# Narrower weights in an attention kernel's value products

## The chip, the cores and the metric

The kernel runs on one core of a Trainium2 chip. The core has a matrix engine (TensorE; PE in the profile, with its weight loads listed apart as PEld), three engines for elementwise work (VectorE or DVE, ScalarE or ACT, GpSimd or POOL), and DMA queues that are fed from ScalarE (ACT) and SyncE (SP). Each engine runs its own list of instructions in order; semaphores order them against each other. The metric is the device time of one execution in microseconds; the median of several runs is compared.

## The reference

There are 16 graphs of 1024 nodes with 256 features and a 0/1 adjacency matrix. Layer 0 is multi-head attention with 8 heads of 32 features, with a leaky ReLU on the scores and the adjacency as mask:

```python
q = heads(features @ Wq); k = heads(features @ Wk); v = heads(features @ Wv)
e = jnp.einsum('whqd,whkd->whqk', q, k)
e = jnp.where(e >= 0, e, ALPHA * e)
attn = jax.nn.softmax(jnp.where(adj[:, None] > 0, e, NEG), axis=-1)
h = jnp.einsum('whqk,whkd->whqd', attn, v)
```

It is followed by a layer norm, a product of `[h, features]` with `Wffn`, another layer norm and a residual. Layer 1 is two graph attention steps (softmax over a sum of two per-node scores, masked by the same adjacency), a layer norm, a feed-forward network with 1024 hidden units, and a last layer norm. All is float32. The change concerns the last line above: weights times values.

## The kernel before

The queries and keys of a head are kept as rows of features, with nodes along the free dimension. Of the 1024 nodes, key tiles of 128 (`t`, 8 of them, `NT`) go on the partitions, and queries in two halves of 512 (`nh`, 2 of them, `NH`) go along the free dimension. The steps of one head are:

- `all_scores` (L576): for two key tiles at a time, 128 keys x 1024 queries of scores into PSUM (`ps_s`).
- `weights` (L594 to L603): `p` = leaky ReLU of the scores (ScalarE scales at L594, VectorE takes the maximum at L596, which also frees the PSUM buffer), its exponential (ScalarE, L599), and the product with the mask (GpSimd, L603). Nothing is subtracted before the exponential.
- `all_values` (L623), the changed step: for two key tiles at a time (`GV`), the values of 128 keys are the stationary operand (the weights of the array), `p` is the moving one, and the result is summed over the 8 key tiles in one PSUM buffer, `acc` (`ps_a` in the profile). There is one such buffer. Queries 0 to 511 land on its partitions from 0, queries 512 to 1023 on those from 64.
- `after_head` (L649 to L656): `acc` is copied to SBUF (`ho`), transposed in blocks of 128 x 128, and the 32 sums are divided by the 33rd.

The values lie in `v` with 33 columns per head (`VW` = `DH` + 1): 32 features and a constant column, so that the 33rd sum is the softmax's denominator (both are negated, and so is the mask). Four heads (`G`) share one `v`, and 31 columns of zeros follow the last of them:

```python
v = buf([P, NT, G * VW + 31], "v", "v")
nc.gpsimd.memset(v[:, :, G * VW:], 0.0)
```

The kernel before reads 64 columns from each head's first, so 31 of them belong to the next head or to the zeros. What they give lands on partitions 33 to 63 and 97 to 127 of `acc`. The copy and the transposes go over all 128 partitions; of the transposed columns only 0 to 32 of each 64 are used:

```python
src = pt.rearrange("p (i j c) -> p j i c", i=TPH, j=NH)
nc.vector.reciprocal(rd, src[:, :, :, DH])
```

The rest of a graph (`rows_pair`, `attention`, `second_rows`, `normed_pair`, `feed_forward`; among their products L847, L872, L912 and L940, and the graph step's exponentials L795 and L797) is worked off while the next graph's heads run, and fills TensorE between their scores and value products.

The order of all instructions is fixed when the program is built. Each piece of work is a thread that names its engine and an estimated cost; a planner (`Order`) picks the next thread by its due time (`aim`) among those that could start soon. The two value tiles of a batch are charged as one piece, `on(PE=240 + 860 * GV)`. Everything is float32; each float32 product of this kernel appears as two weight loads and two matmuls in the profile.

Of the kernel before, what the change touches and what calls it, by code (L numbers as in the profile page):

```python
# [177 lines left out]
def on(shared=False, delay=0.0, **costs):  # L178
    return "on", (costs, shared, delay)
# [6 lines left out]
def wait(event):  # L186
    return "wait", event
# [6 lines left out]
def take(pool):  # L194
    return "take", pool


def give(pool):
    return "give", pool


def start(thread, aim):
    return "start", (thread, aim)


def aim(time, lead):
    return "aim", (time, lead)
# [17 lines left out]
def unshifted_path(  # L225
# [8 lines left out]
    nc = tc.nc  # L234
# [10 lines left out]
    VW = DH + 1  # L245
# [307 lines left out]
    def pace(b):  # L553
        return PACE * {0: AIM["fast0"], 1: AIM["fast1"], B - 1: AIM["fast15"]}.get(b, 1.0)
# [51 lines left out]
    def all_values():  # L606
        for b in range(B):
            for h in range(H):
                g, c = h // G, (h % G) * VW
                for u in range(NP):  # L610
                    yield wait(("v", b, g, u))
                v = vs[b, g]
                yield take("acc")
                acc = psum.tile([P, HALF], FT, tag="acc", name="ps_a", bufs=bufs["acc"])
                for d in range(0, NT, GV):
                    for t in range(d, d + GV):
                        yield wait(("p", b, h, t))
                    yield aim(begin[b] + (h * NT + d + 2) / 2 * pace(b), SLOT)
                    yield on(PE=240 + 860 * GV)
                    for t in range(d, d + GV):  # L620
                        p = probs.pop((b, h, t))
                        for nh in range(NH):
                            nc.tensor.matmul(acc[nh * 64:(nh + 1) * 64, :], v[:, t, c:c + 64],  # L623
                                             p[:, nh * HALF:(nh + 1) * HALF],
                                             start=(t == 0), stop=(t == NT - 1))
                    for t in range(GV):
                        yield give("p")
                yield start(after_head(b, h, acc), begin[b] + (h + 1) * NT // 2 * pace(b))
                if h % G == G - 1:
                    yield give("v")  # L630
            yield start(rest(b), work.now)

    def after_head(b, h, acc):
        if h == 0:
            yield take("hn")
            hn[b] = buf([P, NT, D], "hn", "hn")
            checks[b] = small.tile([P, NSUM + NSCORE], FT, name="check", bufs=2)
            yield fire(("hn open", b))
        yield wait(("hn open", b))
        yield take("pair")  # L640
        ho = buf([P, HALF], "pair", "ho")
        engine = yield evacuate(HALF)
        copy(engine, ho, acc)
        yield give("acc")
        yield take("misc")
        pt = misc()
        yield on(PE=450)
        for i in range(TPH):
            nc.tensor.transpose(pt[:, i * P:(i + 1) * P], ho[:, i * P:(i + 1) * P], ident)  # L649
        yield give("pair")  # L650
        src = pt.rearrange("p (i j c) -> p j i c", i=TPH, j=NH)
        rd = checks[b][:, h * NT:(h + 1) * NT].rearrange("p (j i) -> p j i", j=NH)
        yield on(DVE=210)
        nc.vector.reciprocal(rd, src[:, :, :, DH])
        yield on(DVE=430)
        nc.vector.tensor_tensor(hn[b].rearrange("p (j i) d -> p j i d", j=NH)[:, :, :, h * DH:(h + 1) * DH],  # L656
                                src[:, :, :, :DH], rd[:, :, :, None].to_broadcast([P, NH, TPH, DH]), op=OP.mult)
        yield give("misc")
        yield fire(("hn", b, h))
# [304 lines left out]
    def rest(b):  # L964

        t0 = work.now

        def at(share):
            return t0 + share * SLOT

        for h in range(H):
            yield wait(("hn", b, h))
        yield take("w8")
        y1 = y1s[b] = buf([P, NT, YW], "w8", "y1")
        x1s[b] = dram.tile([NP, P, DC, 2 * P], FT, name="x1_kept")
        for q in range(NH):
            yield start(head_stats(b, q), at(0))
        for u in range(NP):
            yield start(rows_pair(b, u), at(AIM["rows"] + AIM["rows_step"] * u))
        for u in range(NP):  # L980
            yield wait(("hn used", b, u))
        yield give("hn")
        yield start(free_x(b), work.now)
        big = yield from attention(b, 0, y1, at)
        yield take("w8")
        y2 = buf([P, NT, YW], "w8", "y2")
        for i in range(NT):
            yield start(second_rows(b, big, y1, y2, i), at(AIM["second"] + AIM["second_step"] * i))
        for i in range(NT):
            yield wait(("row", b, 1, i))  # L990
        yield give("big")
        yield give("w8")
        for u in range(2):
            yield start(fetch_x1(b, u), at(AIM["normed"]))
        big = yield from attention(b, 1, y2, at)
        yield give("mask")
        yield start(count(b), at(1.0))
        for u in range(NP):
            yield start(normed_pair(b, u, big, y2), at(AIM["normed"] + AIM["normed_step"] * u))
        for u in range(NP):  # L1000
            yield wait(("weighed", b, u))
            if u + 2 < NP:
                yield start(fetch_x1(b, u + 2), at(AIM["normed"]))
        yield give("big")
        yield give("w8")
# [83 lines left out]
    with tc.manual_schedule():  # L1089
        for dst, w in ((wq, Wq), (wk, Wk), (wv, Wv)):  # L1090
            load_w(dst, w)
        work.add(project(0, -SLOT), 0.0)
        work.add(load_stacks(), 0.0)
        work.add(all_scores(), 0.0)
        work.add(all_values(), 0.0)
        work.add(prepare(), 0.5 * SLOT)
        work.run()
# [308 lines left out]
```

## Time and profile before

| | |
|---|---|
| median of three runs | 4535.08 us (4533.97 to 4536.34) |
| the profiled execution | 4533.21 us |
| its span, first to last instruction | 4531.4 us |
| mean granted TensorE clock | 0.987 |
| TensorE busy | 4348.7 us |
| VectorE, ScalarE, GpSimd busy | 3304.5, 2893.6, 2454.6 us |
| L623 matmuls (4096 records) | 1019.9 us busy, 615 ns mean |
| L623 weight loads (4096 records) | 246.1 us busy, 137 ns mean |

The profile is of one execution. Busy time counts a stretch once where records overlap. Matmuls are pipelined, and a record's end is modelled: the time that a matmul really takes from the engine is read from the distance between the starts of neighbouring records, not from the length of one. A weight load overlaps the matmuls that run beside it; what a load costs is again seen in the starts of the matmuls around it. The chain of waits is followed back from the last instruction, at each step to what released it or to the instruction before it on its engine. In lines of instructions, "128*64 128x512" stands for 128 rows and 64 columns of weights and a moving operand of 512 columns.

### The profile page before, as it was taken

To read this page: it belongs to the slowest core of one execution; us is meant where nothing else is said; L and a number is where in the kernel's file an instruction comes from. 1 tells how busy PE (TensorE), PEld (TensorE's weight loads), DVE (VectorE), ACT (ScalarE), POOL (GpSimd) and SP (SyncE) were. 2 spreads that over 40 slices of the span, in tenths; PEclk is the share of its full clock that TensorE was granted. 3 is DMA by queue.
4 is the path that set the end of the run, shared out by engine and by line. 5 is a ranking of instruction groups with operands and counts; after the bars stand their busy time and mean duration, and the time that the engine had idled before them with its cause. 6 is when DMAs were issued, how large, how long until landed. Compare 5 with 4: busy or idle time off the path is not lost.

```text
span 4531.4 us, 57125 instructions
## 1 busy us (share of the span) xinstructions
PE 4348.7 (96%) x20298; PEld 2924.8 (65%) x20298; DVE 3304.5 (73%) x5246; ACT 2893.6 (64%) x4030; POOL 2454.6 (54%) x1544
## 2 busy tenths in 40 slices
PE   6778999999999999999999999999999999999999
PEld 3345666767666676666767666676666767666587
DVE  4766778777787777768777787777768777776854
ACT  4556666666666666666676666666676676666631
POOL 3655565465565545655565565555655565565710
PEclk8899999999999999999999999999999999999999
DMA  5312223222232312323132232322323222231100
GB/s 173 106 49 70 82 70 101 62 79 81 62 98 63 105 54 75 96 59 110 54 89 75 59 98 67 103 64 70 89 64 105 63 86 68 60 99 49 34 22 20
DMA packets 159108, 343.57 MB, mean 76 GB/s; under 512 B 24672, under 2 KB 27232, under 8 KB 158816
## 3 DMA queue, kind: packets, MB, share of 16 engines
q1 hardware_dynamic: 112736, 255.93, 20.0%
q10 hardware_dynamic: 46080, 83.91, 6.2%
q8 instruction: 164, 2.69, 0.2%
q14 instruction: 128, 1.05, 0.1%
HBM read 239.09 MB, written 100.66 MB: 75 GB/s over the span
## 4 chain that ended last, share of the span: by engine, by line
PE 72%; DVE 15%; POOL 5%; issue 4%; ACT 2%; DMA 0%; ACTq 0%; POOLq 0%; SPq 0%; DVEq 0%
PE ps_a L623 16%; PE ps_s L576 10%; PE ps_m L872 8%; PE ps_m L847 8%; PE ps_m L912 7%; PE ps_m L940 7%; DVE att L810 5%; POOL p L603 5%; DVE att L813 5%; PE ps_m L460 3%; DVE p L596 3%; PE ps_m L757 3%; PE ps_m L725 2%; PE ps_m L728 2%; PE ps_m L351 2%
## 5 line engine op out<-in xcount | busy, mean ns | idle before, releaser
L603 POOL TENSOR_TENSOR p<-p,mask 128x1024 f32<-128x1024 f32 x1024 | 2212.3, 2177 | 1654.9 <-ACT p L599 1528.0
L596 DVE TENSOR_TENSOR p<-p,ps_s 128x1024 f32<-128x1024 f32 x1024 | 1209.9, 1213 | 403.0 <-ACT p L594 402.2
L599 ACT ACTIVATE p<-p 128x1024 f32<-128x1024 f32 x1024 | 1081.1, 1058 | 409.7 <-DVE p L596 380.5
L594 ACT ACTIVATE p<-ps_s 128x1024 f32<-128x1024 f32 x993 | 973.6, 1025 | 189.8 <-PE ps_s L576 169.0
L623 PE MATMUL ps_a<-p,v 128*64 128x512 f32 x4096 | 1019.9, 615 | 47.3 <-POOL p L603 45.1
L576 PE MATMUL ps_s<-qs,ks 128*128 128x512 f32 x2048 | 631.5, 428 | 37.2 <-DVE p L596 34.7
L623 PEld LDWEIGHTS ps_a<-p,v 128*64 128x64 f32 x4096 | 246.1, 137 | 536.7 <-issue 384.5
L576 PEld LDWEIGHTS ps_s<-qs,ks 128*128 128x128 f32 x2048 | 352.9, 191 | 331.8 <-DVE p L596 98.3
L872 PE MATMUL ps_m<-y,att 128*128 128x256 f32 x2048 | 483.2, 382 | 16.3 <-ACT v L497 13.6
L940 PE MATMUL ps_m<-wf,hid 128*128 128x256 f32 x2048 | 474.0, 381 | 9.4 <-ACT xT L309 8.7
L912 PE MATMUL ps_m<-rT,wf 128*128 128x256 f32 x2048 | 474.6, 381 | 4.0 <-ACT z L309 4.0
L847 PE MATMUL ps_m<-y,att 128*128 128x258 f32 x2048 | 472.3, 381 | 2.9 <-DVE hn L656 2.9
L872 PEld LDWEIGHTS ps_m<-y,att 128*128 128x128 f32 x2048 | 377.2, 190 | 81.9 <-ACT v L497 16.3
L940 PEld LDWEIGHTS ps_m<-wf,hid 128*128 128x128 f32 x2048 | 379.3, 190 | 78.2 <-issue 15.3
L847 PEld LDWEIGHTS ps_m<-y,att 128*128 128x128 f32 x2048 | 385.9, 190 | 66.7 <-issue 6.0
L912 PEld LDWEIGHTS ps_m<-rT,wf 128*128 128x128 f32 x2048 | 378.6, 191 | 52.7 <-ACT z L309 4.2
L810 DVE SCALAR_TENSOR_TENSOR att<-first,second 128x1024 f32<-128x1024 f32 x256 | 352.7, 1378 | 82.0 <-ACT first L797 82.0
L813 DVE SCALAR_TENSOR_TENSOR att<-mask,att 128x1024 f32<-128x1024 fp8e4 x256 | 329.8, 1288 | 8.7
L818 ACT ACTIVATE y<-y,check 128x258 f32<-128x258 f32 x256 | 130.8, 511 | 299.3 <-DVE check L816 277.7
L334 POOL TENSOR_SCALAR rs<-mv 128x2 f32<-128x2 f32 (+1 forms) x224 | 58.0, 259 | 392.4 <-DVE mv L331 392.3
L400 DVE TENSOR_SCALAR adj_b<-adj_i 128x512 fp8e4<-128x512 int32 x256 | 249.7, 1020 | 15.5 <-DMA adj_i<-in_adj_dram 15.5
L921 ACT ACTIVATE hid<-ps_m,bf 128x256 f32<-128x256 f32 x383 | 163.5, 472 | 130.6 <-PE ps_m L912 102.7
(100 smaller groups left out, 4254.2 us busy)
## 6 DMA issues: line engine op xcount, KB each, us to landing
adj_i<-in_adj_dram ACTq DMA_DIRECT2D x256, 256.0 KB, 3.4
qs<-qk_halves SPq DMA_DIRECT2D x256, 256.0 KB, 4.1
ks<-qk_halves SPq DMA_DIRECT2D x256, 256.0 KB, 5.1
qk_halves<-high SPq DMA_DIRECT2D x128, 256.0 KB, 3.2
qk_halves<-low SPq DMA_DIRECT2D x128, 256.0 KB, 3.7
xr<-in_x_dram ACTq DMA_DIRECT2D x64, 256.0 KB, 2.9
x_kept<-x SPq DMA_DIRECT2D x64, 256.0 KB, 2.0
x<-x_kept SPq DMA_DIRECT2D x64, 256.0 KB, 5.4
```

What stands on the lines that cost most here:

```text
L576: nc.tensor.matmul(ps[i][:, cols], kk[:, t * P:(t + 1) * P], q[:, cols], start=True, stop=True)
L594: nc.scalar.activation(p, ps, AF.Copy, scale=ALPHA)
L596: nc.vector.tensor_tensor(p, p, ps, op=OP.max)
L599: nc.scalar.activation(p, p, AF.Exp)
L603: nc.gpsimd.tensor_tensor(p, p, mask_of(b, t), op=OP.mult)
L623: nc.tensor.matmul(acc[nh * 64:(nh + 1) * 64, :], v[:, t, c:c + 64], p[:, nh * HALF:(nh + 1) * HALF], start=(t == 0), stop=(t == NT - 1))
L810: nc.vector.scalar_tensor_tensor(e, first[:, 0, :], second[:, j:j + 1], first[:, 1, :], op0=OP.mult, op1=OP.max)
L813: nc.vector.scalar_tensor_tensor(e, mask_of(b, j), -1.0, e, op0=OP.mult, op1=OP.mult, accum_out=sums[:, j:j + 1])
L847: nc.tensor.matmul(pa[:, cols:cols + width], big[:, j, i * P:(i + 1) * P], rows[:, j, :width], start=(j == 0), stop=(j == NT - 1))
L872: nc.tensor.matmul(pa[:, i * D:(i + 1) * D], big[:, j, t * P:(t + 1) * P], y2[:, j, :D], start=(j == 0), stop=False)
L912: nc.tensor.matmul(pa[:, i * 2 * P:(i + 1) * 2 * P], wf1[:, dc, hc * P:(hc + 1) * P], rT[:, dc, :], start=(dc == 0), stop=(dc == DC - 1))
L940: nc.tensor.matmul(pa[:, i * D:(i + 1) * D], hid[hc // 2][:, hc % 2, i * P:(i + 1) * P], wf2[:, hc, :], start=(hc == 0), stop=False)
```

## The change

The value product of a head's first key tile stays as it is, with 64 columns of `v` into 64 partitions. For the seven other key tiles it takes `VW` = 33 columns into 33 partitions. The partitions past the 33rd keep what the first tile's product, which begins the sum, put there, and are still copied and transposed. The two query halves keep their first partitions, 0 and 64. The cost that the planner is given is not changed, and the order of instructions is the same on every engine.

```diff
                     for t in range(d, d + GV):
                         p = probs.pop((b, h, t))
                         for nh in range(NH):
-                            nc.tensor.matmul(acc[nh * 64:(nh + 1) * 64, :], v[:, t, c:c + 64],
+
+                            m = VW if t else 64
+                            nc.tensor.matmul(acc[nh * 64:nh * 64 + m, :], v[:, t, c:c + m],
                                              p[:, nh * HALF:(nh + 1) * HALF],
                                              start=(t == 0), stop=(t == NT - 1))
```

## The prediction

> **What bounds the kernel now.** I read the page first: busy shares, the forty slices, the chain that ended last, and the costliest groups.
>
> ```profile
> PE 4348.7 (96%) x20298; PEld 2924.8 (65%) x20298; DVE 3304.5 (73%) x5246; ACT 2893.6 (64%) x4030; POOL 2454.6 (54%) x1544
> ...
> PE   6778999999999999999999999999999999999999
> ...
> PE 72%; DVE 15%; POOL 5%; issue 4%; ACT 2%; DMA 0%; ACTq 0%; POOLq 0%; SPq 0%; DVEq 0%
> PE ps_a L623 16%; PE ps_s L576 10%; PE ps_m L872 8%; PE ps_m L847 8%; PE ps_m L912 7%; PE ps_m L940 7%; DVE att L810 5%; POOL p L603 5%; DVE att L813 5%; PE ps_m L460 3%; DVE p L596 3%; PE ps_m L757 3%; PE ps_m L725 2%; PE ps_m L728 2%; PE ps_m L351 2%
> ```
>
> TensorE is the bound: 96% busy, over 90% in every slice after the fourth, 72% of the chain. The changed line, L623, is the chain's largest entry. The first four slices (some 450 us: graph 0 and most of graph 1) are different: TensorE waits there.
>
> Then I asked for line L623's instructions, and for its place in order of time in a graph in the middle of the run (2001.5 to 2004.9 us; weight loads PEld, then matmuls PE; columns are start, length, and idle time before).
>
> ```profile
> L623 PEld LDWEIGHTS ps_a<-p,v x4096: 132/136/232, 56.5 to 4308.5; 128*64 128x64 f32 x196
> L623 PE MATMUL ps_a<-p,v x4096: 592/592/1116, 56.5 to 4308.9; 128*64 128x512 f32 x196
> ```
> ```profile
> 2001.90 0.20 PEld L623 LDWEIGHTS ps_a<-p,v 128*64 128x64 f32 x4 [0.33 <-issue]
> 2002.39 0.14 PEld L623 LDWEIGHTS ps_a<-p,v 128*64 128x64 f32 x2 [0.29 <-issue]
> 2002.82 0.14 PEld L623 LDWEIGHTS ps_a<-p,v 128*64 128x64 f32 x2 [0.29 <-issue]
> ```
> ```profile
> 2001.90 1.94 PE L623 MATMUL ps_a<-p,v 128*64 128x512 f32 x8
> 2003.77 1.20 PE L576 MATMUL ps_s<-qs,ks 128*128 128x512 f32 x4
> ```
>
> One visit to L623 is a batch: two key tiles by two query halves, and each fp32 product appears as two records, so 8 loads and 8 matmuls. The two halves [...]run together (their starts are 7 ns apart), so a batch is four pairs. The loads at 2002.39 and 2002.82 start with the second and third pair and serve the pair after: each is 0.14 us and lies under 0.43 us of streaming. Only the first load of a batch has no matmul of its own kind to hide under: from the first pair to the second it is 0.49 us here, against 0.43 between the later ones. To the nanosecond the records say 480 against 428, in 500 of the 510 visits. The exposed load is thus 52 ns. A batch takes 2003.77 - 2001.90 = 1.87 us: 4 x 0.428, 0.05 for that load, and about 0.1[...].
>
> [...] The recorded lengths carry a fixed part beside it: medians of 136 ns for 64 columns (above) and 190 for 128 (the page's group of weight loads of L872) differ by 54 for 64 columns, 0.84 ns a column[...]. [...] between the last pair of L623 and the next kind of matmul 522 ns pass, 94 more than a pair's 428; from L847's last (128 columns wide) to L623's first it is 309, 92 more than the 217 between L847's own. That drain is the same within 2 ns after 64 and after 128 columns.
>
> **The change part by part.** Order, number and waits of the instructions stay what they are on every engine, and the planner is charged the same cost, so no transfer moves and no wait is added. [...] Four things can differ:
>
> 1. *Streaming.* 512 moving columns per record, as before: 428 ns a pair. L847 with 128 columns of weights for 258 moving ones has 217, the same 0.84 ns per moving column, so the width of the weights does not enter. Cost 0.
> 2. *Hidden loads.* Three load pairs per batch shorten under a 428 ns cover. Worth 0; without the cover each would show (third rival).
> 3. *First load of a batch.* 31 columns fewer: 31 x 0.84 = 26 ns. A head has 8 key tiles, so 4 batches; the first begins with key tile 0, which keeps 64 columns. That leaves 3 x 128 heads = 384 batches; in the records 382 of them are preceded by other work and so expose the load.
> 4. *Drain after the batch.* The two widths above drain within 2 ns of each other, so 0; half of that difference over 512 batches, 0.5 us either way, bounds it.
>
> Upper end of item 3: 384 x 26 ns = 10.0 us, if TensorE never waited. Lower end: nothing, if 33 columns load no faster than 64. No row shows 33 columns; 64, 128 and also a one-column load late in the run (79 to 82 ns long, on the same line: 80 + 0.84 a column) do, so I take the slope.
>
> How much reaches the end? In the chain in order of time L623 has 16.3% of 4531.4 us, 739 us; by 1.87 us a batch that is 395 of 512 batches, 77%. Counting the batches by the chain itself, 297 of the 382 exposed loads lie on it: 8 of 22 in the first 271 us, 14 of 24 in the last stretch, 19 or 20 of 24 in each graph between. Off the chain a saved 26 ns only makes TensorE wait longer for what ends last there: the weights multiplied by the mask on POOL (L603, of which L623 waits), a score buffer given back by VectorE (L596), or the graph step's exponentials on ScalarE (L795, L797). None of these gets later.
>
> Sum: 297 x 26 ns = 7.7 us. Against the profiled execution: 4533.21 - 7.7 = 4525.5 us, its span from 4531.4 to 4523.7 with the 1.8 us around it unchanged. The median of the runs lies 1.9 us above the profiled one: 4535.08 - 7.7 = **4527.4 us**, 0.17% less. A measurement of this kernel can tell about 0.2% from no change, here 9.1 us (below 4526.0 is faster, above 4544.2 slower), so the likeliest result is on the near side of that line.
>
> **The rivals.**
>
> *All of it arrives.* For it: in a middle graph TensorE is busy 281.5 of 285 us, and its waits there are short, so those charged to VectorE or POOL may themselves move forward once every earlier batch is shorter. Against: the chain does leave TensorE for 4 or 5 batches of each graph, and graph 0 is not bound by it. Time: 4535.1 - 10.0 = 4525.1 us, just over the line.
>
> *The load does not get shorter.* [...] For it: no row has a width that is not a multiple of 32 except that of one column[...]. Against: that one-column record is 80 ns, which lies on the line through 64 and 128[...]. Time: 4535.1 us.
>
> *Slower: the narrow load stops hiding.* The mechanism has its place in the second to fourth pair of a batch[...]. Of those pairs 11 per head have 33 columns (2 in the first batch, 9 in the others), 1408 in all, each showing 27.5 ns: 38.7 us, 30 on the chain at 77%, less 7.7 won. Time: 4535.1 + 22 = 4557 us. It turns the sign once such a pair shows over 10 / 1408 = 7 ns and is slower by more than 0.2% from some 15 ns. For it: nothing in the trace, only that no such width is there. Against: loads of 64 and 128 columns hide alike.
>
> **How the numbers follow.** The likeliest, 7.7 us with between 6.5 and 9.0 by how many batches count: 0.50. All of it arrives, or a little more: 0.30. No gain: 0.12. Slower: 0.08. Faster by over 0.2%: 0.30 and a tenth of the first case's 0.50 (its upper edge touches the line), less 0.01 for those of the second that stay within it: 0.34. Slower 0.08. The rest, 0.58, is within 0.2%. The range: the low end takes in the full 10.0 us and the runs' spread of about 1 us, 4524.2; the high end takes in no gain and that spread, 4536.0. The likeliest's own range is 4526.0 to 4528.6.
>
> **What would show each step.** Loads of 33 columns recorded at 80 + 27.5 = 108 ns, those of 64 (key tile 0) still at 136. First to second pair of a batch about 454 ns where it was 480, in three batches of four; 480 in the first. The other pairs at 428, and 522 from the last pair to the next matmul. A middle graph, from one visit of the feed-forward products to the next at 270.8 us, shorter by about 20 x 26 = 520 ns; by 620 if the first rival holds. The prediction is wrong if the second pair still comes at 480, if the later pairs are over 428, or if the graph's period doesn't follow the batches.

## The result

The changed kernel takes 4526.33 us (median of 20 runs, 4521.36 to 4531.39) against 4532.85 us for the kernel before (20 runs, 4527.64 to 4536.34). The ratio is 0.9985, with a 95% interval of 0.9979 to 0.9991: a small gain, 0.15%, where 0.17% was forecast. By the interval it lies between 4.1 and 9.5 us, so the times alone don't tell 7.7 us from much less; the traces below have to. The profiled execution of the changed kernel took 4521.66 us, among the shortest of its runs, so its whole span is not compared with that of before below.

The page of the changed kernel: busy time, TensorE's slices, and the shares of the chain by engine.

```profile
PE 4333.5 (96%) x20298; PEld 2875.2 (64%) x20298; DVE 3305.8 (73%) x5246; ACT 2893.4 (64%) x4030; POOL 2454.4 (54%) x1544
...
PE   6778999999999999999999999999999999999999
...
PE 69%; DVE 17%; POOL 5%; issue 5%; ACT 3%; DMA 0%; ACTq 0%; POOLq 0%; DVEq 0%
```

TensorE is still the bound, with 15 us less busy time (4348.7 to 4333.5), and it has lost three points of the chain, which VectorE, ScalarE and "issue" have taken. The changed line is now L625. All its instructions (minimum, median and maximum length in ns):

```profile
L625 PEld LDWEIGHTS ps_a<-p,v x4096: 106/111/231, 55.0 to 4297.0; 128*33 128x33 f32 x171, 128*64 128x64 f32 x25
L625 PE MATMUL ps_a<-p,v x4096: 592/592/1117, 55.0 to 4297.4; 128*33 128x512 f32 x171, 128*64 128x512 f32 x25
```

The load's median went from 136 to 111 ns; the matmul's stayed at 592. One batch with 33 columns in order of time, its loads and then its matmuls (start, length, idle before):

```profile
2005.65 0.15 PEld L625 LDWEIGHTS ps_a<-p,v 128*33 128x33 f32 x4 [0.33 <-issue]
2006.11 0.12 PEld L625 LDWEIGHTS ps_a<-p,v 128*33 128x33 f32 x2 [0.31 <-issue]
2006.54 0.12 PEld L625 LDWEIGHTS ps_a<-p,v 128*33 128x33 f32 x2 [0.31 <-issue]
```
```profile
2005.65 1.91 PE L625 MATMUL ps_a<-p,v 128*33 128x512 f32 x8
2007.50 1.19 PE L576 MATMUL ps_s<-qs,ks 128*128 128x512 f32 x4
```

From the first pair to the second it is 0.46 us where it was 0.49, between the later ones 0.43 as before; the batch ends 1.85 us after its start instead of 1.87. To the nanosecond, by the starts of the records in both profiles: 454 in the second, third and fourth batch of a head, 480 in the first; between later pairs 429 in both kernels, and from the last pair to the next product 523 in both. (The prediction has 428 and 522 for these two; its differences stand.)

What a graph gains is best read from its period. In the chain in order of time, the uninterrupted run of 32 feed-forward products recurs once per graph. The kernel before, then the changed one (columns are start and length):

```profile
1137.57 6.98 PE ps_m L912 x32
...
2221.58 6.98 PE ps_m L912 x32
```
```profile
1131.04 6.98 PE ps_m L914 x32
...
2213.58 6.98 PE ps_m L914 x32
```

Four graphs took 1084.01 us and take 1082.54: 0.37 us less for each. Over the twelve periods from graph 3 to graph 15 (graphs are counted from 0), measured at each graph's first value batch, the median went from 271.05 to 270.63 us, 0.42 us.

Where the rest of 24 x 26 ns = 0.62 us went can be followed record by record, since the order is the same. I took the starts of the same matmul in both profiles from the first value batch of graph 6, and listed each place where the difference between them jumps:

| place in graph 6 | jump, ns |
|---|---|
| second pair of the 24 narrowed batches, and two more loads inside a batch | +24 to +27 each, 26 times |
| L649, transposes of head 1's result, which wait for ScalarE's copy | -51 |
| L488, the next graph's value projection, which waits for ScalarE (L497) | -36 |
| L409, mask transposes, which wait for VectorE (L400) | -26 |
| L623, second key tile of a batch, which waits for GpSimd (L603), twice | -25, -25 |
| smaller steps, together | -63 |
| net over the graph | +445 |

Every saved load is there, and the larger losses are at waits of TensorE for another engine. (The changed kernel numbers these lines two higher from L623 on.) In the other middle graphs in which no single wait jumps (see below) the net is 383 to 449 ns. The waits of TensorE's load queue at these places lengthen too (total us, times, longest), before and then after:

```profile
PEld ps_a L623 <- POOL p L603: 127.3, 137, 4.4
...
PEld L409 <- DVE adj_b L400: 21.1, 13, 4.6
...
PEld ps_m L649 <- ACT ho L309: 12.3, 14, 1.5
PEld ps_m L488 <- ACT v L497: 11.9, 17, 1.0
```
```profile
PEld ps_a L625 <- POOL p L603: 138.0, 154, 3.7
...
PEld L409 <- DVE adj_b L400: 21.5, 13, 5.0
...
PEld ps_m L651 <- ACT ho L309: 12.9, 14, 1.5
PEld ps_m L488 <- ACT v L497: 12.6, 17, 1.1
```

The first row grows by far more than the matmuls lose there: their own wait for GpSimd goes from 45.1 to 47.6 us, so most of the longer wait of the loads lay under matmuls that were still running.

### The profile page after: what moved, and what is told of

Same layout as the page of the kernel before. It is cut to its first block, busy times and chain, and to the rows that moved or that the text cites. A ratio compares the mean times of both kernels' runs of the same rounds, so it can differ in the third digit from the quotient of the medians.

```text
span 4519.9 us, 57125 instructions
## 1 busy us (share of the span) xinstructions
PE 4333.5 (96%) x20298; PEld 2875.2 (64%) x20298; DVE 3305.8 (73%) x5246; ACT 2893.4 (64%) x4030; POOL 2454.4 (54%) x1544
## 4 chain that ended last, share of the span: by engine, by line
PE 69%; DVE 17%; POOL 5%; issue 5%; ACT 3%; DMA 0%; ACTq 0%; POOLq 0%; DVEq 0%
PE ps_a L625 15%; PE ps_s L576 9%; PE ps_m L874 7%; PE ps_m L849 7%; PE ps_m L914 7%; PE ps_m L942 6%; POOL p L603 5%; DVE att L812 5%; DVE att L815 5%; DVE p L596 3%; PE ps_m L759 3%; PE ps_m L460 2%; PE ps_m L727 2%; PE ps_m L730 2%; PE ps_m L351 2%
## 5 line engine op out<-in xcount | busy, mean ns | idle before, releaser
L603 POOL TENSOR_TENSOR p<-p,mask 128x1024 f32<-128x1024 f32 x1024 | 2211.6, 2176 | 1645.2 <-ACT p L599 1521.5
L625 PE MATMUL ps_a<-p,v 128*33 128x512 f32 (+1 forms) x4096 | 1005.4, 608 | 49.0 <-POOL p L603 47.6
L625 PEld LDWEIGHTS ps_a<-p,v 128*33 128x33 f32 (+1 forms) x4096 | 198.1, 114 | 560.6 <-issue 398.1
L400 DVE TENSOR_SCALAR adj_b<-adj_i 128x512 fp8e4<-128x512 int32 x256 | 249.4, 1019 | 15.5 <-DMA adj_i<-in_adj_dram 15.5
```

The source lines that it names most:

```text
L603: nc.gpsimd.tensor_tensor(p, p, mask_of(b, t), op=OP.mult)
L625: nc.tensor.matmul(acc[nh * 64:nh * 64 + m, :], v[:, t, c:c + m], p[:, nh * HALF:(nh + 1) * HALF], start=(t == 0), stop=(t == NT - 1))
```

## The experiments

The theory: each narrowed first load saves 26 ns on TensorE; those that the chain passes by (it runs through another engine there) are given back at the next wait, the others reach the end. The chain of the changed kernel passes by seven of the 24 narrowed batches of a middle graph (head and batch within it, both from 0: 1,2; 1,3; 2,1; 4,1; 4,2; 4,3; 5,1). The rival: every load returns the same share, wherever it stands.

**Wide again in the seven off the chain.**

```diff
-                            m = VW if t else 64
+                            off = ((1, 2), (1, 3), (2, 1), (4, 1), (4, 2), (4, 3), (5, 1))
+                            m = VW if t and (h, d // GV) not in off else 64
```

> Seven of the 24 narrowed first loads of a head cycle (head, batch: 1,2; 1,3; 2,1; 4,1; 4,2; 4,3; 5,1) go back to 64 columns: those that the chain of the changed kernel passes by. Theory (what is saved there is given back at a wait of TensorE soon after): the period of a graph, from the third graph's first value batch to the fifteenth's over 12, stays at the changed kernel's 270.58 us. Rival (every load saved returns the same 69% of its 26 ns, wherever it is): 0.125 us longer, 270.71.

**Narrow in those seven alone.** The same list, with `in` for `not in`.

> The mirror: 33 columns in those seven batches alone, 64 in all others. Theory: the period is that of the kernel before, 271.01 us, although each of the seven first loads is 26 ns shorter. Rival: 0.125 us shorter, 270.88.

**Wide again in seven on the chain.** The same as the first, with another list.

> The control: seven batches that lie on the chain (0,1; 1,1; 2,2; 3,2; 5,3; 6,2; 7,3) go back to 64 columns. Theory: all seven count, 7 x 26 = 182 ns, period 270.58 + 0.18 = 270.76 us. Rival: 270.71. What tells them apart is the difference to the run with the other seven wide: 0.18 us by the theory, 0 by the rival.

The chain in order of time of the first and of the third:

```profile
1132.24 6.98 PE ps_m L915 x32
...
2214.97 6.98 PE ps_m L915 x32
```
```profile
1132.88 6.98 PE ps_m L915 x32
...
2215.98 6.98 PE ps_m L915 x32
```

Over these four graphs the period is 270.68 us with the off-chain seven wide and 270.78 with the on-chain seven wide. The expectations name the mean over twelve periods (graphs 3 to 15 here). It is not a clean measure, since single graphs stand out. By about 0.3 us: graphs 3 and 9 by waits that only they have, and others because the product at L460, which waits for VectorE, starts 0.23 us earlier in some graphs than in others. By 1.0 us: where TensorE's clock drops (last section). The mean gives 270.72, 271.29 and 270.82 us for the three. The median over the twelve sets the jumps aside. In the profiles that bear on this:

| kernel | median period, us |
|---|---|
| before (three profiles) | 271.05, 271.09, 271.10 |
| narrow in the off-chain seven alone | 271.04 |
| wide in the on-chain seven | 270.78 |
| wide in the off-chain seven | 270.67 |
| changed (two profiles) | 270.63, 270.71 |

By the medians, widening the seven off the chain costs nothing beyond the scatter of the changed kernel itself, and narrowing them alone gains at most what before scatters. Widening seven on the chain costs 0.07 to 0.15 us, less than the 0.18 expected. By the means that the expectations name, the first run would have spoken for the rival and the second for neither.

The record by record comparison with the changed kernel decides it more finely. Seven middle graphs (4 to 8, 11 and 12) have no jump in any of the three profiles. In each of them the off-chain seven, nine loads with the two that a wait inside a batch exposes, save some 233 ns and return a net of -12 to 83, 32 on average. The on-chain seven save 182 and return 97 to 167, 137 on average. So the place decides, though off the chain about a seventh of the saving still arrives on average, and on it about three quarters, not all.

**Other widths.** 40, 48 and 56 columns in the second to fourth batch of each head.

```diff
-                            m = VW if t else 64
+                            m = (64, 64, 40, 40, 48, 48, 56, 56)[t]
```

> Widths of 40, 48 and 56 columns in the second, third and fourth batch of each head. If the load takes 0.84 ns a column, the second pair of a batch follows the first by 460, 467 and 473 ns (480 at 64, 454 at 33). If it goes in steps of 16 columns: 467, 467, 480; if what counts is only that the width isn't 64, 454 in all three. The period by the chain: 5 x 20 + 6 x 13 + 6 x 7 = 0.22 us shorter than before, 270.79 us.

Measured: 460, 467 and 473 ns, and a median period of 270.82 us (270.79 expected). With 454 at 33 and 480 at 64 these five lie on one line of 0.84 ns a column. The steps of 16 columns in the expectation are out, and so is the second rival of the prediction, that the load gets no shorter.

**The changed kernel again, and a version with one wide product in all.**

> The changed kernel once more, beside the next one on the same chip. By the graphs' periods it should gain 0.43 us in each of the last fourteen graphs, 6.0 us, and 0.6 us in the first two: 4526.3 us by the last median of before, ratio 0.9985. If the gain sat in a luckier start of the one profiled run, the period in this profile would be that of before, 271.0 us.

Measured: 4526.49 us against 4532.65, ratio 0.9987 (0.9980 to 0.9994). The gain repeats. Its median period is 270.71 us, not 271.0: the gain is in the graphs.

```diff
     def all_values():
+        acc = psum.tile([P, HALF], FT, tag="acc", name="ps_a", bufs=bufs["acc"])
         for b in range(B):
...
-                acc = psum.tile([P, HALF], FT, tag="acc", name="ps_a", bufs=bufs["acc"])
...
-                            m = VW if t else 64
+                            m = VW if t or (b, h) != (0, 0) else 64
```

> 64 columns in the very first value product of the program alone; every other one takes 33, so the first batch of each later head exposes a short load too. Upper partitions of the one sum buffer keep finite numbers from the first head. Theory: 8 more first loads of 26 ns per graph, six of them on the chain (those of heads 2 and 5 are off it), 0.156 us a graph: period 270.43 us (median of graphs 270.47), and 2.4 us under the changed kernel, ratio 0.998 to before. Rival (no more to be had, the other engines are next): period as the changed kernel's.

Measured: 4523.86 us, ratio 0.9983 (0.9974 to 0.9992), median period 270.53 us. Its chain, from the same place:

```profile
1130.22 6.98 PE ps_m L914 x32
...
2211.99 6.98 PE ps_m L914 x32
```

That is 270.44 us for each of these four graphs. The medians, 0.10 to 0.18 us under the changed kernel's two, agree with six loads of 26 ns, 0.156. Record by record, in the five of the seven graphs above that have no jump here either (4, 6, 7, 8 and 12), the eight loads save 24 to 27 ns each and 100 to 139 arrive, a little less than six loads' worth. This edit also takes 26 semaphore instructions out of TensorE's list (941 to 915 in the trace), but in these graphs every step of over 20 ns in its favour stands at a second pair of a batch, so the gain is the loads'. It has the lowest median of all kernels here; its interval against before overlaps that of the changed kernel, so the 2.6 us between those two rest on the periods.

**Fewer visits.** The wide-once version with four key tiles per batch, with 6 and with 5 buffers for `p`. The planner's charge follows `GV`, so the order of instructions changes too, and with it which engine makes some of the copies. The diff is that of 6 buffers, without the lines of the wide-once version; with 5, `p` and `pair` stay as they were.

```diff
-    GV = 2
+    GV = 4
...
-    bufs = dict(misc=3, scores=2, acc=1, p=5, stacks=2, stage=2, adj=2, adjb=2, pair=18,
+    bufs = dict(misc=3, scores=2, acc=1, p=6, stacks=2, stage=2, adj=2, adjb=2, pair=16,
```

> As the run before, with four key tiles per visit to the value products instead of two (6 buffers for the weights instead of 5, 16 instead of 18 of the small ones, to make room). It halves the visits, 256 fewer, and each visit costs two drains of 0.09 us and an exposed load of 0.027: 0.21 us, 54 us in all, 4479 us at 80% on the chain: 4490. Rival: four finished weight tiles at a time of six buffers starve the scores, TensorE waits for GpSimd at the value line, and the time is longer than before.

> Four key tiles per visit with the buffers left as they are (5 and 18). If buffers for the weights are what limits the longer visit, it is slower than the run with 6 buffers, by the wait of TensorE at the value line for GpSimd; if not, both take about the same.

Measured: 4726.5 us (ratio 1.0427, 1.0411 to 1.0443) and 5280.98 us (1.1650, 1.1629 to 1.1671). The expectation of 4490 us was wrong, and the rival was right on the sign. Its place was wrong: the matmuls of the value line wait 4.5 us for GpSimd in the version with 6 buffers, against 47.6 in the changed kernel, and TensorE waits most at the scores, for VectorE to free a score buffer. The matmul waits of the version with 6 buffers (total us, times, longest), and the same wait in the changed kernel:

```profile
PE ps_s L576 <- DVE p L596: 145.3, 105, 9.1
```
```profile
PE ps_s L576 <- DVE p L596: 35.3, 25, 10.4
```

VectorE frees a score buffer only after it has a `p` to write to; that these are held longer by the longer visit is the likely cause, argued from the code and from the fact that 5 buffers are slower than 6, with 240.5 us at that wait. It is not shown, for VectorE also has more to do. With 6 buffers the page says:

```profile
PE 4360.3 (92%) x20298; PEld 2932.8 (62%) x20298; DVE 3415.4 (72%) x5338; ACT 2850.6 (60%) x3938; POOL 2521.1 (53%) x1544
```

The new order gives VectorE 92 instructions that ScalarE had, and it is busy 110 us longer than in the changed kernel. No run here keeps the old order, so the two causes are not parted. Within a longer visit the pairs follow each other every 429 ns, without the 523 ns to another product and the 454 or 480 ns after it in the middle. Two batches that meet without a wait show the same (16 matmuls from 130.35 us on in the profile of before, from 128.79 in that of the changed kernel): after a first spacing of 480 and 454 ns all others are 429 or 430. That saving is real, but neither of these two kernels gets it.

**The opening.** In the profiles so far TensorE's clock was at half for less time before 610 us in the narrow kernels, and graph 2 began earlier. Two kernels split the change by graph, and before was profiled twice more.

```diff
-                            m = VW if t else 64
+                            m = VW if t and b < 2 else 64
```

> 33 columns in the first two graphs alone, 64 from the third on. In the profiles so far TensorE ran at half clock for 109 to 113 us of the first 610 in the three kernels that are wide or nearly so, and for 92 to 96 us in the five that are narrow; the third graph began at 544.8 to 547.2 us against 540.8 to 542.9. Theory (the shorter loads also move work out of half-clock windows in the opening): the third graph begins at about 542.4 us, with 96 us at half clock before 610, and the time falls by some 3.6 us. Rival (what the sum on record says of these two graphs): 0.6 us less and the third graph at 545.5 or later. Both: later periods as before, median 271.05.

The mirror has `b >= 2`.

> The mirror: 64 columns in the first two graphs, 33 in the value products from the third graph on. Theory: half clock for 109 us or more before 610, the third graph at about 546 us, periods of 270.63 to 270.71 (median), so 14 x 0.35 to 0.42 = 4.9 to 5.9 us off the time. Rival (the opening's clock has nothing to do with the loads): 96 us at half clock or a value in between as often as not.

> The kernel before, profiled again for how much of a profile repeats. If the opening's half-clock windows belong to the kernel: 109 us again and the third graph at 545 to 547 us; median period 271.05. If they belong to the run, they scatter.

> The same a third time: 109 us at half clock before 610 and a median period of 271.05 us, if they belong to the kernel. Half-clock windows after 610 us, of which the first profile had none and the others up to seven, scatter in either case.

| kernel | half clock before 610 us, us | graph 2 begins, us | ratio to before |
|---|---|---|---|
| before, first profile | 109.2 | 547.2 | |
| before, second | 85.3 | 540.4 | |
| before, third | 109.2 | 546.0 | |
| narrow in graphs 0 and 1 | 95.6 | 541.2 | 0.9998 (0.9989 to 1.0007) |
| narrow from graph 2 on | 109.2 | 545.9 | 0.9992 (0.9984 to 1.0001) |
| changed, two profiles | 95.6, 95.6 | 541.6, 542.9 | 0.9985, 0.9987 |

The second profile of before falls out of the pattern: 85 us at half clock, and a start of graph 2 as early as that of any narrow kernel. So the early opening does not belong to the narrow loads alone. It also doesn't keep its lead: in that execution the last graph's value batches took 251.2 us from first to last, in the other two of before 247.7. The kernel that is narrow in graphs 0 and 1 starts graph 2 early and has 251.3. My theory that the change shortens the opening by some 3.6 us is not borne out, nor excluded: the first kernel of this pair gains 0.9 us by its ratio (2.4 by the medians), which fits the 0.6 of the prediction as well, and its interval, from 5.0 less to 3.2 more, holds both. The other part, from graph 2 on, has 3.6 us by its ratio (4.1 by the medians), 4.9 to 5.9 expected, with an interval that reaches from 7.3 less to 0.5 more. The median periods of the two, 271.06 and 270.66 us, are those of before and of the changed kernel, as expected, so the gain in the later graphs is shown by the periods. What the first two graphs give is left open.

## Why the prediction was right

- *The bound and the place* held: of L623 the width shortened the first load of a batch, and beside it only a load that follows a late tile (below).
- *The price*, 26 ns a load, held to the nanosecond: 480 to 454. Streaming, the hidden loads and the step from the last pair to the next product cost nothing, as said: 429 and 523 are the same in both kernels. ("Drain" in the prediction and in an expectation is a name for the 94 ns between these two; what fills them was not shown.) The recorded length of a load of 33 columns has a median of 111 ns, where 108 was forecast; at 0.84 ns a column the 27.5 in that sum is 27.7.
- *The count* was a little too high. The sum had 19 or 20 batches of a middle graph on the chain, some 0.52 us a graph, taken from the chain of the kernel before; the chain of the changed kernel has 17 in nearly every middle graph, and 17 x 26 = 0.44 us is close to what the periods show (0.41 between the means of the medians above: 271.08 and 270.67). Part of the difference is how I counted: batch 4,1, and 4,3 in 9 graphs of 13, lie in a stretch that the chain of before calls "issue", and I took those for TensorE's own. The other part is that the chain moved: batch 1,2 was off it in 4 of 13 graphs before and in all 13 after, 4,3 in 9 and then 13. A count of batches is a fair estimate and no more: the experiments show some three quarters of a saving arrive on the chain and a seventh off it, so that 17 x 26 comes so near is in part luck.
- *What is given back* was named as GpSimd's masks, VectorE's score buffers and ScalarE's exponentials. In the records it is GpSimd's masks, ScalarE's copies (L309, L497) and VectorE's masks (L400). The kind was right; two of the three places were not. Nor had I seen that a batch whose second tile arrives late exposes a second load: two per graph, 26 instead of 24.
- *The sum*: 7.7 us predicted, 6.5 and 6.2 by the two pairs of medians. The graphs from 2 on give 14 x 0.41 = 5.7, where the sum had about 7; the term that was mis-sized is the share on the chain. The predicted time, 4527.4, was set from a median of 4535.08 over three runs, which more runs put at 4532.65 to 4533.27. That the time came within 1.1 us is luck: a base 2.2 us too high and a gain 1.2 us too large partly cancel. The range, 4524.2 to 4536.0, took in everything from the full 10.0 us to no gain, so a time inside it says little; the spacings and the periods are the test.
- *The rivals.* All of it arrives: no, 0.41 of 0.62 us a graph. The load gets no shorter: no, 454 ns where it was 480. The narrow load stops hiding: no, later pairs stay at 429 ns.

## What to carry to other kernels

In this kernel the cost of a weight load was what it put between the starts of matmuls, not its recorded length: loads of 33 and 64 columns were recorded at 111 and 136 ns and showed as 25 and 51 (454 and 480 against 429). Of four load pairs in a batch only the one after other work showed, and one whose tile came late; these showed by their columns, 26 ns for 31. In a kernel whose engines are nearly balanced, multiply a saving by its share of the chain, and expect somewhat less, since the saving itself moves the chain: here the chain of before promised 0.52 us a graph, and 0.41 came. When a gain is smaller than the spread of runs, compare the period of a repeating stage in the traces, by medians and record by record.

## What the runs showed of the hardware

TensorE's clock dropped to half for single stretches of 3.4 us in the middle of the run too, where it is busy 98% of the time (3636 to 3640 of the 3700 us from 610 to 4310 in the profiles of before and of the changed kernel). In the twelve profiles of kernels with two key tiles a batch there are six such stretches between 610 and 4100 us: three in the kernel that is narrow in the off-chain seven alone, two in the second profile of the changed kernel, one in the kernel that is narrow from graph 2 on, and none in the others, among them all three of before. (From 4148 us on, in the last graph, most profiles have one or two more, some 6.8 us long.) All six stand at one place of a graph, 172.0 to 172.5 us after its first value batch, just after the second of two waits for ScalarE. In the second profile of the changed kernel one begins at 1246.1 us (the mean granted clock from 1245 to 1249 us is 0.63); the matmuls (start, length, idle before):

```profile
1243.74 1.16 PE L488 MATMUL ps_m<-wv,xT 128*128 128x128 f32 x8 [0.57 <-ACT v L497]
1245.89 3.65 PE L874 MATMUL ps_m<-y,att 128*128 128x256 f32 x8 [1.00 <-ACT v L497]
...
1250.33 1.89 PE L874 MATMUL ps_m<-y,att 128*128 128x256 f32 x8
```

Eight products take 3.65 us where the next eight take 1.89, and that graph's period is 271.70 us where its neighbours have 270.97 and 270.73. The same waits stand in every graph, and mostly the clock holds. When a stretch begins does not follow from the waits alone: in each of the twelve profiles all half-clock stretches, the opening's too, start a whole number of 3.413 us apart. In the six graphs the second wait ended 0.15 to 0.47 us before such a point. In eight other graphs it did so as well, and they kept the full clock, so what else it takes stays open.

The spread of the times goes with the clock: the changed kernel's 20 runs have 4531.1 us on average at a mean clock of 0.985 (two runs) and 4521.9 at 0.989 (four), more between them than the change is worth. The mean counts the opening and the last graph too, so the six stretches are only a part of that.
